# A graph network layer pair on Trainium2: unordered scatters of the edge list, and list steps tied behind given messages

## The chip, the cores and the metric

One core of a Trainium2 chip runs the whole program. The metric is the device time of one execution in microseconds. The engines are named as in the profile: PE (TensorE matmul; PEld its weight loads), DVE (VectorE), ACT (ScalarE), POOL (GpSimd) and SP (SyncE); SPq, ACTq and POOLq are the queues from which an engine issues DMAs.

## What is computed

There are 6250 nodes with 256 features and 106250 edges, sorted by destination; 6250 of them are self loops and the others come in both directions. Two layers run one after the other on the same edges. Layer 0 sends a message over each edge, which depends on the source node and on one of two edge types; layer 1 is a graph attention layer with four heads. Cut to what matters (`norm` is a layer norm without weights):

```python
def edge_nn(x, W, b):
    h = relu(x @ W.T + b)
    return relu(h @ W.T + b)
msgs = where(rel == r, edge_nn(x[src], W_rel[r], b_rel[r]), ...)   # r = 0, 1
agg = segment_sum(msgs, dst)
i, f, g, o = split(agg @ W_ih.T + b_ih + b_hh, 4)
hn = sigmoid(o) * tanh(sigmoid(i) * tanh(g))
x = norm(x + mlp3(hn))                       # three small dense layers
...
h = x @ W                                    # 4 heads of 64
e = leaky_relu(a_src[src] + a_dst[dst], 0.2)
alpha = softmax of e over the edges of each dst
y = norm_affine(segment_sum(alpha * h[src], dst) + bias + x)
x = norm(x + relu(y))
```

## The kernel before

The kernel has a first stage, which this change touches, and a long second part (`fast`), which it doesn't. (A slower path, `general`, is there for inputs whose edges aren't sorted as expected; the profiled run doesn't take it.)

**Messages.** A message depends on source and type only, so there are just 2 x 6250 different ones. They are computed once per node and type and stored in device memory as the table `parts0`. Nodes are taken in 49 blocks of 128 (`NB = 49`); a "message" below is the message block of one such block, both types. The loop at L1138 takes pieces of four blocks (`CHUNK = 4`); with 49 blocks the last piece has one. For each piece SP loads the transposed features `fxc` (L1141, three buffers), PE makes the hidden layer with eight products into `fph` (L1149), ACT adds the bias and applies relu (L1156); then for each block PE makes four products into `fpm` (L1163, two PSUM buffers), DVE adds the bias (`fms`, L1171, three buffers), ACT applies relu (L1174) and SP stores the block (L1176).

**The edge list.** Beside that, DVE takes the edge list apart. SP loads destinations, sources and types (L810 to L833). From L839 on DVE packs source, type and flags of an edge in one word, drops the self loops by moving the words left in seven rounds (the loop from L879, `frame` and `moved`), and works out where each block of 64 words goes (`place`). POOL then writes 21 groups of blocks (seven parts of the list by three blocks) to `packed` in device memory with indirect DMAs (L931). `packed` has been filled with zeros by a DMA from ACT (L805), and the blocks that the scatters write lie apart: blocks of odd and even rows go to two halves. SP reads the two halves back in six DMAs (L961, L965, L970: `both` and `low`). DVE joins them and splits the fields again (L975 to L1048): rows of the message table (`frow`), destinations (`list_f`), flags (`frel_f`), sources (`fsrc`), steps of the destination (`fstep`); SP stores the steps as `cuts` (L1034). PE turns these five lists with 35 transpositions (L1059), DVE copies the results to `fidx` (twice), `dstE`, `fmark` and `ffirst` (L1064, L1072). One small product (L1085, `low_p`) spreads the first destinations of the windows over the partitions, one (L1076) adds up checks. Seven more transpositions (L1129) turn `fslot`, ACT copies each to `rel_b` (L1133, two buffers) and SP stores it in `slots` (L1134).

**What sets the order.** In this first stage a scheduler puts the instructions of each engine in one fixed order when the program is built, and adds the waits that the data need; it starts from the program text, in which the whole list comes ahead of the messages. Each engine and each issuing queue works in its order: an instruction that waits holds up all that stand behind it. Two DMAs that write the same tensor are ordered, unless the program says that they need not be. The order of the second part is written out by hand.

**The second part.** After a branch on `odd_i`, 782 gathers on POOL (L1271) fetch rows of `parts0`, PE sums them by one-hot products (L1633), and the dense part of layer 0 follows in between; then 782 gathers of `rows` and the attention layer. The first gather waits for the last message store.

Of the kernel before, what the change touches and what calls it, by code (L numbers as in the profile page):

```python
# [42 lines left out]
P = 128  # L43
# [6 lines left out]
NB = -(-N // P)  # L50
# [6 lines left out]
CHUNK = 4  # L57
# [17 lines left out]
NC = -(-EC // CT)  # L75
# [628 lines left out]
def gnn_kernel(  # L704
# [26 lines left out]
    nc = tc.nc  # L731

    def at(ap, offset, dims):
        return bass.AP(tensor=ap.tensor, offset=ap.offset + offset, ap=dims)

    def rows(ap, n):

        return at(ap, 0, [[0, P], [1, n]])
# [4 lines left out]
    slots = dram.tile([NW, (WT + 1) * P], BF16, name="slots")  # L743
    cuts = dram.tile([(NC + 1) * CT, P], F32, name="cuts")
    kept = dram.tile([NG, P, 3 * D], F32, name="kept")
    packed = dram.tile([2 * BLOCKS, HB], I32, name="packed")
# [25 lines left out]
    with (  # L772
# [2 lines left out]
        tc.tile_pool(name="fmsgp", bufs=2, space=PSUM) as mps,  # L775
    ):
        WrT_s = mw.tile([P, 2, 2, D], F32, name="fWrT")
        nc.scalar.dma_start(WrT_s, WrT.rearrange("r (k p) f -> p r k f", p=P))
        brc = mw.tile([P, 2, 2], F32, name="fbrc")
        brr = mw.tile([P, 2 * D], F32, name="fbrr")  # L780
        with nc.allow_non_contiguous_dma(reason="bias vectors, one element a partition"):
            nc.scalar.dma_start(brc, br.rearrange("r (k p) -> p r k", p=P))
        nc.scalar.dma_start(brr, rows(br, 2 * D))
        zrow = mw.tile([1, D], F32, name="fzrow")
        nc.vector.memset(zrow, 0.0)
        nc.sync.dma_start(parts0[ZERO0 : ZERO0 + 1, :], zrow)

        with (
# [19 lines left out]
            rest = EC - (NC - 1) * CT  # L808
            whole = CT * P
# [43 lines left out]
            work = lp.tile([P, NC, P], F32, name="work")  # L853
# [25 lines left out]
            for b in range(7):  # L879
                s = 1 << b  # L880
# [44 lines left out]
            for b in range(3):  # L925
                nc.vector.tensor_scalar(
                    place[:, b, :], two_t, side, float(b), op0=OP.add, op1=OP.add
                )
            for k in range(NC):
                for b in range(3):  # L930
                    nc.gpsimd.indirect_dma_start(  # L931
                        out=packed,
                        out_offset=bass.IndirectOffsetOnAxis(ap=place[:CT, b, k : k + 1], axis=0),
                        in_=frame[:CT, k, b * HB : (b + 1) * HB],
                        in_offset=None,
                    )


# [15 lines left out]
            both = lp.tile([P, 2, NC, P + 1], I32, name="both")  # L954
            nc.gpsimd.memset(both[:, :, NC - 1, :], 0)
            low_2 = lp.tile([1, 2, NW + 1], I32, name="low_2")
            nc.gpsimd.memset(low_2, 0)
            rest = TC - (NC - 1) * CT
            for s in range(2):
                o = (s * BLOCKS + 1) * HB - 1  # L960
                nc.sync.dma_start(  # L961
                    both[:CT, s, : NC - 1, :],
                    at(packed, o, [[P, CT], [whole, NC - 1], [1, P + 1]]),
                )
                nc.sync.dma_start(  # L965
                    both[:rest, s, NC - 1, :],
                    at(packed, o + (NC - 1) * whole, [[P, rest], [1, P + 1]]),
                )
                with nc.allow_non_contiguous_dma(reason="the last edge before each window"):
                    nc.sync.dma_start(  # L970
                        low_2[:, s, 1:NW], at(packed, o + WT * P, [[0, 1], [WT * P, NW - 1]])
                    )

            low_r = lp.tile([1, NW + 1], I32, name="low_r")
# [31 lines left out]
            for none, to, of in (  # L1006
# [24 lines left out]
            steps = step[:, :, :P]  # L1031
            nc.vector.tensor_sub(steps[:CT], list_f[:CT, :, 1:], list_f[:CT, :, :P])
            nc.vector.tensor_scalar(work[:CT], steps[:CT], FAR, None, op0=OP.mult)
            nc.sync.dma_start(  # L1034
                cuts[: NC * CT, :].rearrange("(k p) e -> p k e", p=CT), work[:CT, :, :]
            )
            far = lp.tile([CT, P], F32, name="far")
            nc.vector.memset(far, FAR)
# [5 lines left out]


            dstE = lp.tile([P, COLS], F32, name="dstE")
            src0 = src1
            nc.vector.tensor_scalar(src0[:CT], src1[:CT], 1.0, None, op0=OP.subtract)  # L1048
            for to, of in (
                (idx0, row),  # L1050
                (dstE, list_f[:, :, 1:]),
                (mark, rel_f[:, :, :P]),
                (idx1, src0),
                (first, steps),
            ):
                for k0, kn in blocks_of(NC, 4):
                    pt = lps.tile([P, 4 * CT], F32, name="turned")
                    for k in range(kn):
                        nc.tensor.transpose(  # L1059
                            pt[:, k * CT : (k + 1) * CT], of[:CT, k0 + k, :], ident[:CT, :CT]  # L1060
                        )
                    n = min(kn * CT, COLS - k0 * CT)
                    if to is not mark:
                        nc.vector.tensor_copy(to[:, k0 * CT : k0 * CT + n], pt[:, :n])  # L1064
                        continue

                    to2, of2 = (
                        ap.rearrange("p (g j) -> p g j", j=2 * WT)
                        for ap in (mark[:, k0 * CT : k0 * CT + n], pt[:, :n])
                    )  # L1070
                    for a, b, c in ((0, 1, 0), (1, 2, WT), (2, WT + 1, 1), (WT + 1, 2 * WT, WT + 1)):
                        nc.vector.tensor_copy(to2[:, :, a:b], of2[:, :, c : c + b - a])  # L1072
# [9 lines left out]
            nc.vector.tensor_scalar(odd_i, odd[:, 6:7], 1.0, None, op0=OP.min)  # L1082

            low_p = lps.tile([P, NW + 1], F32, name="low_p", bufs=1)
            nc.tensor.matmul(low_p, ones[0:1, :], low, start=True, stop=True)  # L1085
            low_b = lp.tile([P, NW + 1], F32, name="low_b")
            nc.vector.tensor_copy(low_b, low_p)
            own = dstE[:, : NW * WT].rearrange("p (w j) -> p w j", j=WT)
# [37 lines left out]
            for w0, wn in blocks_of(NW, P // (WT + 1)):  # L1126
                pt = lps.tile([P, 4 * CT], F32, name="turned")
                n = wn * (WT + 1)
                nc.tensor.transpose(  # L1129
                    pt[:n, :P], slot[:, w0 : w0 + wn, :].rearrange("p w j -> p (w j)"), ident  # L1130
                )
                rel_b = lp.tile([P, P], BF16, name="rel_b", bufs=2)
                nc.scalar.copy(rel_b[:n, :], pt[:n, :P])  # L1133
                nc.sync.dma_start(  # L1134
                    slots[w0 : w0 + wn, :].rearrange("w (j e) -> (w j) e", e=P), rel_b[:n, :]
                )

        for b0, bn in blocks_of(NB, CHUNK):  # L1138
            cols = bn * P
            xc = mp.tile([P, 2, CHUNK * P], F32, name="fxc", bufs=3)  # L1140
            nc.sync.dma_start(  # L1141
                xc[:, :, :cols], xT[:, b0 * P : b0 * P + cols].rearrange("(k p) n -> p k n", p=P)
            )
            hT = mp.tile([P, 2, 2, CHUNK * P], F32, name="fhT")
            for r in range(2):
                for m in range(2):
                    ph = mps.tile([P, CHUNK * P], F32, name="fph")
                    for k in range(2):
                        nc.tensor.matmul(  # L1149
                            ph[:, :cols],  # L1150
                            WrT_s[:, r, k, m * P : (m + 1) * P],
                            xc[:, k, :cols],
                            start=(k == 0),
                            stop=(k == 1),
                        )
                    nc.scalar.activation(  # L1156
                        hT[:, r, m, :cols], ph[:, :cols], AF.Relu, bias=brc[:, r, m : m + 1]
                    )
            for j in range(bn):
                pm = mps.tile([P, 2, D], F32, name="fpm")  # L1160
                for r in range(2):
                    for k in range(2):
                        nc.tensor.matmul(  # L1163
                            pm[:, r, :],
                            hT[:, r, k, j * P : (j + 1) * P],
                            WrT_s[:, r, k, :],
                            start=(k == 0),
                            stop=(k == 1),
                        )
                ms = mp.tile([P, 2, D], F32, name="fms", bufs=3)  # L1170
                nc.vector.tensor_add(  # L1171
                    ms.rearrange("p r f -> p (r f)"), pm.rearrange("p r f -> p (r f)"), brr
                )
                nc.scalar.activation(ms, ms, AF.Relu)  # L1174
                b = b0 + j
                nc.sync.dma_start(  # L1176
                    parts0[2 * b * P : 2 * (b + 1) * P, :].rearrange("(p r) f -> p (r f)", r=2),
                    ms.rearrange("p r f -> p (r f)"),
                )

    odd_v = nc.values_load_multi_w_load_instructions(
        odd_i,
# [855 lines left out]
```

## Time and profile before

| what | us |
|---|---|
| timed, median of 3 runs (lowest, highest) | 2273.53 (2273.02, 2274.97) |
| the profiled execution, its own time | 3062.77 |
| its span, first to last instruction | 3061.0 |
| first product of the messages starts | 6.18 |
| first scatter to last scatter starts | 77.85 to 135.11 |
| list reload issues | 137.37 to 141.01 |
| last message product ends | 199.16 |
| first gather of layer 0 starts | 203.84 |
| last gather of layer 0, first gather of layer 1 | 1434.05, 1482.51 |
| last gather of layer 1 starts | 2969.30 |

The profiled execution is much longer than the timed ones. Its page gives busy time of each engine (PE 1529.9, DVE 1229.8, POOL 1527.2), groups of instructions with the idle time before them and what ended most of it, and the trace behind it answers with timelines and waits. A row of a timeline has the start, the duration, the engine, the line, the operation, what it writes and reads, how often, and in brackets the idle time before it with its releaser. Matmuls of 32-bit floats have two records each, so that `x16` are eight products.

### The profile page before, as it was taken

The numbers are of one execution on the slowest core, as the hardware profiler recorded it, in microseconds if no ns is written. First come the engines' busy times: TensorE is split into PE (matmuls) and PEld (weight loads), VectorE is DVE, ScalarE is ACT, GpSimd is POOL, SyncE is SP. The second block draws the span as 40 slices with busy tenths as digits, with TensorE's granted clock in tenths as the row PEclk, the third lists the DMA queues.
The fourth block names the chain that finished last, engine by engine and source line by source line (L and its number), as shares of the span: only waits on it lengthen the run. The fifth ranks groups of instructions, "written<-read, shape, count | busy, mean of one in ns | idle before, by whom it ended". The sixth has DMA issues, their size and how long they took to land. (4 is left out here: it accounts for less than half of the span.)

```text
span 3061.0 us, 22029 instructions
## 1 busy us (share of the span) xinstructions
PE 1529.9 (50%) x5722; PEld 792.0 (26%) x5722; DVE 1229.8 (40%) x3333; ACT 506.0 (17%) x1526; POOL 1527.2 (50%) x1603
## 2 busy tenths in 40 slices
PE   9871276767676756788223332423324233242344
PEld 5540132323233322334111111212112121121222
DVE  8240132322333233333114544535445354453656
ACT  3320011211121211134201111111111111111112
POOL 0227566666666666641473354553545545455440
PEclk9985688878788878889555665656656566565667
DMA  4343334444444434442342243342433334243330
GB/s 150 109 137 108 96 104 122 143 124 139 132 139 135 131 118 132 131 127 79 100 117 79 80 116 86 103 108 81 117 84 106 105 83 117 82 111 100 88 99 27
DMA packets 163393, 332.53 MB, mean 109 GB/s; under 512 B 42451, under 2 KB 74290, under 8 KB 163257
## 3 DMA queue, kind: packets, MB, share of 16 engines
q0 software_dynamic: 75968, 208.00, 24.6%
q1 hardware_dynamic: 64736, 82.92, 8.4%
q10 hardware_dynamic: 22553, 40.12, 4.3%
q8 instruction: 47, 0.77, 0.1%
q14 instruction: 89, 0.73, 0.1%
HBM read 278.79 MB, written 52.12 MB: 108 GB/s over the span
## 5 line engine op out<-in xcount | busy, mean ns | idle before, releaser
L1271 POOL DMA_INDIRECT G<-rows,fidx x782 | 743.9, 951 | 746.6 <-DVE gw L1818 513.3
L1271 POOL DMA_INDIRECT G<-parts,fidx x782 | 752.3, 962 | 483.9 <-issue 216.4
L1927 PE MATMUL fps<-gw,oh 128*64 128x264 f32 (+1 forms) x1674 | 448.2, 480 | 284.1 <-DVE gw L1818 218.1
L1633 PE MATMUL fps<-G,oh 128*64 128x257 f32 (+1 forms) x1674 | 465.2, 428 | 91.5 <-issue 49.7
L1927 PEld LDWEIGHTS fps<-gw,oh 128*64 128x64 f32 (+1 forms) x1674 | 233.9, 171 | 468.6 <-DVE gw L1818 231.7
L1818 DVE TENSOR_TENSOR gw<-G,bank 128x1792 f32<-128x1792 f32 (+1 forms) x167 | 249.1, 1491 | 169.8 <-issue 123.7
L1633 PEld LDWEIGHTS fps<-G,oh 128*64 128x64 f32 (+1 forms) x1674 | 204.1, 152 | 332.1 <-issue 219.8
L1777 PE MATMUL turn<-s,toward 120*120 120x1 f32 (+2 forms) x60 | 15.7, 331 | 435.9 <-DVE s L1774 432.4
L1486 PE MATMUL fpg<-faT,fWihT 128*128 128x512 f32 (+2 forms) x432 | 182.9, 549 | 49.2 <-issue 28.7
L1773 DVE TENSOR_TENSOR_SCAN s<-cut,turn 120x128 f32<-120x128 f32 (+2 forms) x30 | 12.6, 419 | 448.1 <-remote 442.6
L1439 DVE TENSOR_SCALAR kind<-fps 128x1 f32<-128x1 f32 x112 | 12.4, 152 | 359.6 <-PE fps L1633 183.8
L1454 PE MATMUL fpg<-fident,agg 128*128 128x128 f32 x112 | 29.2, 351 | 236.7 <-DVE agg L1443 132.7
L1354 DVE TENSOR_TENSOR oh<-bank,fslot 128x1024 f32<-128x1024 f32 x112 | 136.1, 1215 | 0.6 <-ACT bank L1797 0.6
L1777 PEld LDWEIGHTS turn<-s,toward 120*120 120x120 f32 (+2 forms) x60 | 13.2, 278 | 450.2 <-DVE s L1774 445.9
L1766 PE MATMUL turn<-fident,e 128*120 128x128 f32 (+2 forms) x30 | 13.5, 449 | 229.3 <-issue 214.6
L1594 DVE COPY nd<-hr 128x4 f32<-128x4 f32 x56 | 9.8, 176 | 242.6 <-ACT hr L1573 150.4
L1486 PEld LDWEIGHTS fpg<-faT,fWihT 128*128 128x128 f32 x432 | 73.8, 198 | 124.0 <-issue 96.7
L1149 PE MATMUL fph<-fxc,fWrT 128*128 128x512 f32 (+1 forms) x208 | 91.7, 589 | 6.3 <-DMA fWrT<-in_WrT_dram 6.2
L1163 PE MATMUL fpm<-fWrT,fhT 128*128 128x256 f32 x392 | 89.1, 381 | 0.6 <-DVE fms L1171 0.5
L1867 ACT ACTIVATE frs<-fmv,eps_c 128x1 f32<-128x1 f32 x112 | 33.0, 294 | 332.0 <-DVE fmv L1866 121.9
L1457 DVE COPY faT<-fpg 128x256 f32<-128x256 f32 x56 | 23.6, 422 | 157.0 <-remote 72.6
L1779 ACT COPY ends<-turn 120x2 f32<-120x2 f32 (+2 forms) x30 | 4.8, 159 | 493.2 <-PE turn L1778 478.1
(237 smaller groups left out, 1964.7 us busy)
## 6 DMA issues: line engine op xcount, KB each, us to landing
kept<-keep SPq DMA_DIRECT2D x56, 384.0 KB
k<-kept ACTq DMA_DIRECT2D x56, 384.0 KB
dB<-slots ACTq DMA_DIRECT2D x112, 128.0 KB
loop<-parts SPq DMA_DIRECT2D x110, 128.0 KB
parts<-fms SPq DMA_DIRECT2D x49, 256.0 KB
G<-parts,fidx POOLq DMA_INDIRECT x782
G<-rows,fidx POOLq DMA_INDIRECT x782
rows<-hr SPq DMA_DIRECT2D x110, 65.0 KB
```

The source lines that it names most:

```text
L1149: nc.tensor.matmul(ph[:, :cols], WrT_s[:, r, k, m * P : (m + 1) * P], xc[:, k, :cols], start=(k == 0), stop=(k == 1),)
L1163: nc.tensor.matmul(pm[:, r, :], hT[:, r, k, j * P : (j + 1) * P], WrT_s[:, r, k, :], start=(k == 0), stop=(k == 1),)
L1271: nc.gpsimd.indirect_dma_start(out=to_tile, out_offset=None, in_=table, in_offset=bass.IndirectOffsetOnAxis(ap=idx, axis=0),)
L1354: nc.vector.tensor_tensor(to[:, :nj, :], iota_s[:, None, :].to_broadcast([P, nj, SLOTS]), of[:, :, None].to_broadcast([P, nj, SLOTS]), op= ...
L1454: nc.tensor.transpose(pt[:, k * P : (k + 1) * P], agg[:, k * P : (k + 1) * P], ident)
L1457: nc.vector.tensor_copy(aT[:, :, i * P : (i + 1) * P], pt.rearrange("p (k n) -> p k n", k=2))
L1486: nc.tensor.matmul(pg[:, :cols], WihT_s[:, k, c * P : (c + 1) * P], aT[:, k, :cols], start=(k == 0), stop=(k == 1),)
L1633: nc.tensor.matmul(sums[g][to, :], ohj, got[t], start=begins, stop=ends)
L1777: nc.tensor.matmul(pd[:rs, 0:1], toward[:rs, 0, :rs], b[:, P - 1 : P], start=True, stop=True)
L1818: nc.vector.tensor_mul(gw[:, :, :D].rearrange("p j (h f) -> p j h f", h=H), of[:, :n, :D].rearrange("p j (h f) -> p j h f", h=H), ex[:, o ...
L1867: nc.scalar.activation(r, mv[u, k, 1:2], AF.Ln, bias=eps_c[u])
L1927: nc.tensor.matmul(sums[g][to, :], ohj, gw, start=begins, stop=ends)
```

## The change

It does these things:

- The weights `fWrT` are loaded in two DMAs, type 0 first, the biases between them; the table of ACT functions is loaded ahead of the first use (`preload_act_table_set`).
- The message loop begins with a piece of one block and goes on with twelve of four.
- The 21 scatters are declared free of order among themselves. The six DMAs of the reload are made to wait for all 21.
- Steps of the list get a place in the order of their queue or engine: the reload comes behind the store of message 29 (`NB - 20`), the store of `cuts` behind that of 38, the stores of `slots` behind that of 45; the transpositions of the five lists come behind the products of messages 35 to 39, and `low_p` behind those of 35. These ties (`NoSync`) set an order and add no wait of their own.
- `rel_b` has seven buffers instead of two.

```diff
@@ -775,12 +775,15 @@
         WrT_s = mw.tile([P, 2, 2, D], F32, name="fWrT")
-        nc.scalar.dma_start(WrT_s, WrT.rearrange("r (k p) f -> p r k f", p=P))
         brc = mw.tile([P, 2, 2], F32, name="fbrc")
         brr = mw.tile([P, 2 * D], F32, name="fbrr")
-        with nc.allow_non_contiguous_dma(reason="bias vectors, one element a partition"):
-            nc.scalar.dma_start(brc, br.rearrange("r (k p) -> p r k", p=P))
+        for r in range(2):
+            nc.scalar.dma_start(WrT_s[:, r, :, :], WrT[r].rearrange("(k p) f -> p k f", p=P))
+            if r == 0:
+                with nc.allow_non_contiguous_dma(reason="bias vectors, one element a partition"):
+                    nc.scalar.dma_start(brc, br.rearrange("r (k p) -> p r k", p=P))
         nc.scalar.dma_start(brr, rows(br, 2 * D))
+        nc.scalar.preload_act_table_set("exp_and_others")
@@ -926,13 +929,31 @@
+            moves, behind = [], []
             for k in range(NC):
                 for b in range(3):
-                    nc.gpsimd.indirect_dma_start(
+                    move = nc.gpsimd.indirect_dma_start(
                         out=packed,
...
                     )
+                    for other in moves:
+                        tc.declare_no_dep(move.ins, other.ins, reason="blocks of their own")
+                    moves.append(move)
+
+            def after_moves(load):
+                behind.append((NB - 20, load))
+                for move in moves:
+                    tc.add_manual_dep(
+                        load.ins,
+                        move.ins.name,
+                        mybir.DependencyInfo(
+                            mybir.DependencyClass.Sync, mybir.DependencyReason.DATA
+                        ),
+                        reason="the whole list",
                     )
@@ -958,17 +979,23 @@
-                nc.sync.dma_start(
-                    both[:CT, s, : NC - 1, :],
-                    at(packed, o, [[P, CT], [whole, NC - 1], [1, P + 1]]),
-                )
+                after_moves(
+                    nc.sync.dma_start(
+                        both[:CT, s, : NC - 1, :],
+                        at(packed, o, [[P, CT], [whole, NC - 1], [1, P + 1]]),
+                    )
+                )
...
@@ -1031,8 +1058,13 @@
-            nc.sync.dma_start(
-                cuts[: NC * CT, :].rearrange("(k p) e -> p k e", p=CT), work[:CT, :, :]
+            behind.append(
+                (
+                    NB - 11,
+                    nc.sync.dma_start(
+                        cuts[: NC * CT, :].rearrange("(k p) e -> p k e", p=CT), work[:CT, :, :]
+                    ),
+                )
             )
@@ -1056,9 +1089,11 @@
                     for k in range(kn):
-                        nc.tensor.transpose(
+                        turn = nc.tensor.transpose(
                             pt[:, k * CT : (k + 1) * CT], of[:CT, k0 + k, :], ident[:CT, :CT]
                         )
+                        late.append((turns // 2, turn))
+                    turns += 1
@@ -1082,7 +1117,7 @@
-            nc.tensor.matmul(low_p, ones[0:1, :], low, start=True, stop=True)
+            late.append((0, nc.tensor.matmul(low_p, ones[0:1, :], low, start=True, stop=True)))
@@ -1129,13 +1164,20 @@
-                rel_b = lp.tile([P, P], BF16, name="rel_b", bufs=2)
+                rel_b = lp.tile([P, P], BF16, name="rel_b", bufs=7)
                 nc.scalar.copy(rel_b[:n, :], pt[:n, :P])
...
+                behind.append(
+                    (
+                        NB - 4,
+                        nc.sync.dma_start(
+                            slots[w0 : w0 + wn, :].rearrange("w (j e) -> (w j) e", e=P),
+                            rel_b[:n, :],
+                        ),
+                    )
+                )
-        for b0, bn in blocks_of(NB, CHUNK):
+        for b0, bn in [(0, 1)] + [(1 + b, n) for b, n in blocks_of(NB - 1, CHUNK)]:
@@ -1160,7 +1202,7 @@
-                        nc.tensor.matmul(
+                        made = nc.tensor.matmul(
@@ -1173,10 +1215,24 @@
-                nc.sync.dma_start(
+                store = nc.sync.dma_start(
...
+                tied = [(NB - 14 + n, one, made) for n, one in late]
+                tied += [(n, one, store) for n, one in behind]
+                for n, one, sooner in tied:
+                    if b == n:
+                        tc.add_manual_dep(
+                            one.ins,
+                            sooner.ins.name,
+                            mybir.DependencyInfo(
+                                mybir.DependencyClass.NoSync, mybir.DependencyReason.DATA
+                            ),
+                            reason="the list comes late",
+                        )
```

More of the change, by code (lines that the diff above doesn't have):

```diff
@@ L960, in gnn_kernel @@
                 o = (s * BLOCKS + 1) * HB - 1
-                nc.sync.dma_start(
-                    both[:CT, s, : NC - 1, :],
-                    at(packed, o, [[P, CT], [whole, NC - 1], [1, P + 1]]),
-                )
-                nc.sync.dma_start(
-                    both[:rest, s, NC - 1, :],
-                    at(packed, o + (NC - 1) * whole, [[P, rest], [1, P + 1]]),
+                after_moves(
[3 more added lines that the diff above has]
+                    )
+                )
+                after_moves(
+                    nc.sync.dma_start(
+                        both[:rest, s, NC - 1, :],
+                        at(packed, o + (NC - 1) * whole, [[P, rest], [1, P + 1]]),
+                    )
                 )
                 with nc.allow_non_contiguous_dma(reason="the last edge before each window"):
-                    nc.sync.dma_start(
-                        low_2[:, s, 1:NW], at(packed, o + WT * P, [[0, 1], [WT * P, NW - 1]])
+                    after_moves(
+                        nc.sync.dma_start(
+                            low_2[:, s, 1:NW], at(packed, o + WT * P, [[0, 1], [WT * P, NW - 1]])
+                        )
                     )
@@ L1033, in gnn_kernel @@
             nc.vector.tensor_scalar(work[:CT], steps[:CT], FAR, None, op0=OP.mult)
-            nc.sync.dma_start(
-                cuts[: NC * CT, :].rearrange("(k p) e -> p k e", p=CT), work[:CT, :, :]
+            behind.append(
+                (
+                    NB - 11,
+                    nc.sync.dma_start(
+                        cuts[: NC * CT, :].rearrange("(k p) e -> p k e", p=CT), work[:CT, :, :]
+                    ),
+                )
             )
@@ L1046, in gnn_kernel @@
             dstE = lp.tile([P, COLS], F32, name="dstE")
+            late, turns = [], 0
             src0 = src1
@@ L1131, in gnn_kernel @@
                 )
-                rel_b = lp.tile([P, P], BF16, name="rel_b", bufs=2)
+                rel_b = lp.tile([P, P], BF16, name="rel_b", bufs=7)
                 nc.scalar.copy(rel_b[:n, :], pt[:n, :P])
-                nc.sync.dma_start(
-                    slots[w0 : w0 + wn, :].rearrange("w (j e) -> (w j) e", e=P), rel_b[:n, :]
+                behind.append(
+                    (
+                        NB - 4,
+                        nc.sync.dma_start(
+                            slots[w0 : w0 + wn, :].rearrange("w (j e) -> (w j) e", e=P),
+                            rel_b[:n, :],
+                        ),
+                    )
                 )
-        for b0, bn in blocks_of(NB, CHUNK):
+        for b0, bn in [(0, 1)] + [(1 + b, n) for b, n in blocks_of(NB - 1, CHUNK)]:
             cols = bn * P
@@ L1175, in gnn_kernel @@
                 b = b0 + j
-                nc.sync.dma_start(
+                store = nc.sync.dma_start(
                     parts0[2 * b * P : 2 * (b + 1) * P, :].rearrange("(p r) f -> p (r f)", r=2),
@@ L1179, in gnn_kernel @@
                 )
+                tied = [(NB - 14 + n, one, made) for n, one in late]
[9 more added lines that the diff above has]
+                            reason="the list comes late",
+                        )
     odd_v = nc.values_load_multi_w_load_instructions(
```

## The prediction

> **What bounds the kernel now.** I read the page first, for the shape of the whole. Two groups of gathers on POOL stand on top, 782 each:
>
> ```profile
> span 3061.0 us, 22029 instructions
> L1271 POOL DMA_INDIRECT G<-rows,fidx x782 | 743.9, 951 | 746.6 <-DVE gw L1818 513.3
> L1271 POOL DMA_INDIRECT G<-parts,fidx x782 | 752.3, 962 | 483.9 <-issue 216.4
> ```
>
> In the timeline of POOL undisturbed gathers start 1.25 us apart (204 on, 600 on, 1482 on). 1564 x 1.25 = 1955; with the first gather at 203.84, 47 us between the layers (1435 to 1482.5) and 91 us after the last gather (2970 to 3061) this makes 2297, against 2273.53 timed. So the timed runs have hardly any of the gathers' idle time that the profile has (3062.77 for that execution), POOL paces them nearly from 204 to the end, and what comes before the first gather stands wholly on the path. The change touches only that stretch, so the whole sum is made there. Next I read the timelines of PE, DVE, POOL and SP's queue from 0 to 205, then the queue's waits. PE:
>
> ```profile
> 6.18 9.20 PE L1149 MATMUL fph<-fxc,fWrT 128*128 128x512 f32 x16 [6.18 <-DMA fWrT<-in_WrT_dram]
> ...
> 99.30 7.07 PE L1163 MATMUL fpm<-fWrT,fhT 128*128 128x256 f32 x32
> ...
> 113.07 7.07 PE L1163 MATMUL fpm<-fWrT,fhT 128*128 128x256 f32 x32
> ...
> 133.75 1.88 PE L1149 MATMUL fph<-fxc,fWrT 128*128 128x512 f32 x4
> 146.39 0.77 PE L1085 MATMUL low_p<-low,fones 1*128 1x113 f32 x2 [10.76 <-DVE low L980]
> ...
> 158.34 0.97 PE L1059 MATMUL turned<-fident,frow 126*128 126x126 f32 x7 [0.82 <-DVE frow L1026]
> ...
> 197.27 1.89 PE L1163 MATMUL fpm<-fWrT,fhT 128*128 128x256 f32 x8
> ```
>
> A piece of four messages takes 13.77 us (99.30 to 113.07) and PE is dense, but for one hole of 10.76 (the bracket: idle time before the row, and what ended it). What made it, from the timelines of DVE and of POOL and the waits of SP's queue:
>
> ```profile
> 130.56 0.69 DVE L1171 TENSOR_TENSOR fms<-fpm,fbrr 128x512 f32<-128x512 f32 x1 [1.09 <-PE fpm L1163]
> 143.09 1.10 DVE L992 TENSOR_TENSOR both<-both 126x903 int32<-126x903 int32 x1 [11.84 <-DMA both<-packed]
> ...
> 158.22 0.14 DVE L1043 TENSOR_REDUCE bad<-same 126x1 f32<-126x7 f32 x1
> ```
> ```profile
> 77.85 1.16 POOL L931 DMA_INDIRECT packed<-frame,place  x1 [70.98 <-DVE fms L1171]
> 80.84 1.00 POOL L931 DMA_INDIRECT packed<-frame,place  x1 [1.83 <-DMA packed<-frame,place]
> ...
> 135.11 0.99 POOL L931 DMA_INDIRECT packed<-frame,place  x1 [1.51 <-DMA packed<-frame,place]
> 203.84 0.99 POOL L1271 DMA_INDIRECT G<-parts,fidx  x1 [67.74 <-ACT G L1654]
> ```
> ```profile
> SPq L961 <- DMA packed<-frame,place: 15.3, 1, 15.3
> ```
>
> Read backwards: PE waits for the list's lows from DVE, DVE for the list's reload, the reload (SP, 137.37 to 141.01) for the scatters, and each of 21 scatters for the one before to land: 57.3 us over 20 steps, 2.86 each, 2.46 where nothing else is in flight. The store of messages behind the reload waits too.
>
> PE's account: twelve pieces 165.2, the last one-message piece 4.4, the list's transpositions and small products 7.3; sum 176.9, against 193.0 from 6.18 to 199.16. The 16.1 between are 10.76 + 0.82 for the list, 2.3 of slow first matmuls (9.20 instead of 6.9), 1.3 at 41 while DVE unpacks, 0.9 of crumbs.
>
> **What the Trainium skill says.** "DMA: Bandwidth & Descriptors", section "Anatomy of one DMA — SWDGE (gpsimd) path": some 2.0 us fixed for each, mostly the receipt of the write, and the issuing sequencer does any waiting. The trace agrees in kind: 0.99 on POOL, then 1.5 or more of waiting. "TensorE: Matmul & The Clock Gate", "Part 1: The HAM clock gate": about the first 3.4 us run at half clock; here the first weight loads stand 0.86 apart until 10.0 and 0.43 later. "ScalarE: Activation LUTs", "What ACT_TABLE_LOAD costs": 1.28 us; the trace has 1.28, from 6.92.
>
> **The change, part by part**, with the instruction order of the built kernel beside the trace's durations.
>
> *Start.* The first piece has one message: its columns (128 KB) and half the weights (256 KB) instead of 512 KB each stand ahead of the first matmul. 1 MB landed at 6.18, some 5 us after issue; half of it, with a fixed part left, gives an estimate of 4.6. The piece takes 4.4 warm and 2.0 more for the slow clock: message 0 done at 11.0. The last piece now has four messages, so PE's work is the same. The preloaded table takes 1.28 off ACT, where it waited for the biases till 6.92 while PE needed it at 9.6 only: nothing, except for the small piece that needs it sooner. Against the gain: SP's fourth column load now waits for PE's first piece (about 9.2) and stands before the ten list loads, which started at 6.21. Unpacking on DVE then has no gain: 59.8 us of dense work (17.1 to 76.9), ended near 77 to 78 as before. PE loses some 1.9 to it. So the start brings about 1 us, between -2 and 2.
>
> *Scatters.* Twenty waits of 1.5 to 3.5 go[...]. The pitch becomes POOL's own, 1.25 as in the gathers: 20 x 1.25 = 25, so landed near 106 instead of 137. The trace has no unordered scatters of this kind; bounds are 1.25 and the old 2.86.
>
> *Reload.* Tied behind the store of message 29. Messages 0 to 32 end at T = 11.0 + 8 x 13.77 + 1.9 = 123.1; message 29 at 117.9, its store (sum, relu, 1.6) at 119.5; six issues of 3.6 (137.37 to 141.01) and 2.1 to land: 125.2. Behind them wait the stores of messages 30 to 32; sums have three buffers, and DVE turns to the list next, so nothing waits for these.
>
> *List on DVE.* In the new order it stands after the sum of message 32, 32 instructions in one block, 15.3 us as in the trace (143.09 to 158.36): 125.2 to 140.5. Then message 33's sum, 0.7. PE meanwhile has 8 first products (6.9), messages 33 and 34 (3.5) and 6 more first products (5.2), to T + 15.5 = 138.6, then needs that sum: a hole of 2.6 in place of 10.76 + 0.82.
>
> *Transpositions* stand behind messages 35 to 39, so each group finds DVE's input ready. Walking through in order, PE waits 0.2 for a copy and about 1.0 for the slots: copies between them are DVE work of 13.6 us, beside 15 us and more of PE's. If that cover were gone, 3 us. Their time on PE is unchanged. Stores of cuts and slots move back in SP's queue, behind messages 38 and 45; seven buffers let ACT go on, and they land well before the first gather.
>
> *Sum.* T + 4 pieces 55.1 + small products 7.0 + holes 3.8 = 189.0, against 199.16: 10 us in the profiled execution (3062.77 to 3053). After it, 4.7 us to the first gather, unchanged.
>
> For the timed runs I take less. The hole is made of the scatters' landing times. At the 2.46 that the trace shows without company they end 8 us sooner, and the hole shrinks from 10.8 to 2.8: the gain is then 2. The extra steps stand beside message loads and stores, which timed runs have too, so I expect most, not all, of the hole: 6.5 us, 2273.5 - 6.5 = 2267.0.
>
> **Rivals.**
> 1. *The hole is small in the timed runs* (scatters at 2.3 to 2.5): 0 to 4.5 gained, 2271. For it: 790 us of the profiled time are absent from timed runs, so the profile slows something. Against: the loads and stores of this stretch land within about 2 us even there.
> 2. *Scatters stay serial though nothing orders them* (the ring drains one at a time): the change then doesn't do what it says. SP reaches the reload at 119.5 and blocks, with every message store behind it. At 2.86 they land at 137.2, the list starts at 143, PE gets message 33's sum at 159 instead of 141: 18 later, 8 slower than before, 2281. It decides from a pitch of about 2.5 on. Against: gathers run at 1.25 with many in flight.
> 3. *The list comes too late at the start*: the blocked list loads hold unpacking up by 3 to 5 us, and PE idles with it; gain and loss cancel, 2273 to 2277.
>
> **How the numbers follow.** Forecast 0.55 (its own range 2263 to 2269), rival 1 0.33, rival 2 0.06, rival 3 0.06, of which a third beyond 0.2%. 0.2% is 4.5 us, about what a measurement of this kernel can tell from no change. Faster 0.55, same 0.37, slower 0.08. The range from 2263 to 2274.5 leaves out gains above 10.5 (0.06), rival 2 and half of rival 3.
>
> **What would show it.** In the profile after: 21 scatters 1.25 to 1.4 apart, ended before 110; reload near 120 without a wait; low product after message 35 without a wait; one PE hole of 2 to 4 us near 139; first gather near 194. Wrong if scatters stay near 2.5, if the first gather moves by under 3 us, or if the unpack ends after 80. If the first gather is 10 sooner and the time isn't, the hole was the profiler's.

## The result, and the profile after

| what | before | after |
|---|---|---|
| timed, median of 8 runs each (lowest, highest), us | 2275.27 (2273.02, 2277.97) | 2268.24 (2265.01, 2271.69) |
| ratio to before, 95% interval | | 0.9969 (0.996 to 0.9979) |
| profiled execution, own time and span, us | 2276.0, 2274.2 (taken again, e0 below) | 2266.64, 2264.7 |
| first scatter to last scatter starts | 77.97 to 136.28 | 78.33 to 104.34 |
| list reload issues | 138.53 to 142.16 | 121.28 to 125.03 |
| last message product ends | 200.36 | 190.25 |
| first gather of layer 0 starts | 205.04 | 194.91 |

The change gained 7.0 us (4.8 to 9.1 by the interval). The kernel before takes some 2275 us in some executions and 3050 to 3060 in others (its first profile, and six of the twelve runs below), so each time is set only against the runs of before made beside it, whose median is given.

From the page of after, the span and the two groups of gathers (busy, mean ns, idle before them):

```profile
span 2264.7 us, 22022 instructions
L1327 POOL DMA_INDIRECT G<-parts,fidx x782 | 747.1, 955 | 327.5 <-issue 219.0
L1327 POOL DMA_INDIRECT G<-rows,fidx x782 | 747.5, 956 | 240.5 <-issue 222.9
```

The gathers idle 568 us here, where the first profile of before had 1230: this span is near the timed runs, that one was not. The timeline of POOL (start, duration, and in brackets the idle time before the row):

```profile
78.33 1.21 POOL L937 DMA_INDIRECT packed<-frame,place  x1 [71.54 <-DVE frame L902]
79.84 0.99 POOL L937 DMA_INDIRECT packed<-frame,place  x1 [0.30 <-issue]
...
104.34 0.98 POOL L937 DMA_INDIRECT packed<-frame,place  x1 [0.30 <-issue]
194.91 0.99 POOL L1327 DMA_INDIRECT G<-parts,fidx  x1 [89.58 <-ACT G L1710]
```

Twenty steps take 26.0 us, 1.30 each, in place of 58.3 in e0. No scatter's bracket names a landing any more. SP's queue and then DVE, both from their timelines:

```profile
120.63 0.33 SPq L1218 DMA_DIRECT2D parts<-fms  x1
121.28 0.35 SPq L983 DMA_DIRECT2D both<-packed  x1
```
```profile
124.49 0.69 DVE L1213 TENSOR_TENSOR fms<-fpm,fbrr 128x512 f32<-128x512 f32 x1 [1.03 <-PE fpm L1205]
127.20 1.10 DVE L1019 TENSOR_TENSOR both<-both 126x903 int32<-126x903 int32 x1 [2.02 <-DMA both<-packed]
...
142.39 1.27 DVE L1213 TENSOR_TENSOR fms<-fpm,fbrr 128x512 f32<-128x512 f32 x2
```

The reload follows the store of message 29 at once, and no wait for the scatters is left among the waits of SP's queue. DVE waits 2.0 for the rows instead of 12.9 (e0; 11.8 in the first profile of before), then makes no sum until 142.39. What that does to PE, from its timeline:

```profile
4.72 3.78 PE L1191 MATMUL fph<-fxc,fWrT 128*128 128x128 f32 x16 [4.72 <-DMA fWrT<-in_WrT_dram]
...
134.55 5.31 PE L1191 MATMUL fph<-fxc,fWrT 128*128 128x512 f32 x12
143.12 3.11 PE L1205 MATMUL fpm<-fWrT,fhT 128*128 128x256 f32 x8 [3.25 <-DVE fms L1213]
146.02 1.52 PE L1092 MATMUL turned<-fident,frow 126*128 126x126 f32 x7
147.47 0.47 PE L1120 MATMUL low_p<-low,fones 1*128 1x113 f32 x2
...
183.18 7.07 PE L1205 MATMUL fpm<-fWrT,fhT 128*128 128x256 f32 x32
```

One hole of 3.25 is left, with another releaser: not the list itself, but the sum of message 33, which stands behind the list on DVE. The small product and the transpositions, which waited 10.76 and 0.82 in the first profile of before, follow without a bracket.

### The profile page after: what moved, and what is told of

It reads as the page before. It is cut to its first block, busy times and chain, and to the rows that moved or that the text cites. A ratio compares the mean times of both kernels' runs of the same rounds, so it can differ in the third digit from the quotient of the medians.

```text
span 2264.7 us, 22022 instructions
## 1 busy us (share of the span) xinstructions
PE 1556.6 (69%) x5722; PEld 776.5 (34%) x5722; DVE 1237.3 (55%) x3333; ACT 508.5 (22%) x1526; POOL 1525.5 (67%) x1603
## 3 DMA queue, kind: packets, MB, share of 16 engines
q1 hardware_dynamic: 64736, 82.92, 11.4%
## 5 line engine op out<-in xcount | busy, mean ns | idle before, releaser
L1689 PE MATMUL fps<-G,oh 128*64 128x257 f32 (+1 forms) x1674 | 533.1, 433 | 137.1 <-DMA G<-parts,fidx 120.6
L1983 PE MATMUL fps<-gw,oh 128*64 128x264 f32 (+1 forms) x1674 | 433.0, 469 | 238.3 <-DVE gw L1874 238.3
L1689 PEld LDWEIGHTS fps<-G,oh 128*64 128x64 f32 (+1 forms) x1674 | 196.6, 151 | 445.5 <-DMA G<-parts,fidx 226.7
L1495 DVE TENSOR_SCALAR kind<-fps 128x1 f32<-128x1 f32 x112 | 12.5, 153 | 311.1 <-PE fps L1689 311.1
L1542 PE MATMUL fpg<-faT,fWihT 128*128 128x512 f32 (+2 forms) x432 | 171.6, 521 | 0.2 <-DVE faT L1513 0.2
L1929 ACT ACTIVATE fy<-fy,frs 128x256 f32<-128x256 f32 x112 | 67.2, 600 | 98.4 <-DVE gw L1868 52.9
L1205 PEld LDWEIGHTS fpm<-fWrT,fhT 128*128 128x128 f32 x392 | 74.9, 194 | 23.8 <-DVE fms L1213 8.8
L1873 ACT COPY gw<-bank 128x28 f32<-128x28 f32 (+1 forms) x167 | 28.5, 171 | 227.6 <-DMA dB<-slots 103.6
L1625 PE MATMUL fpg<-Wx,fyT 128*128 128x264 f32 x224 | 77.0, 474 | 3.0 <-ACT fyT L1616 3.0
L937 POOL DMA_INDIRECT packed<-frame,place x21 | 20.9, 995 | 77.6 <-DVE frame L902 71.5
```

Of the source, the lines that this page charges most:

```text
L1205: made = nc.tensor.matmul(pm[:, r, :], hT[:, r, k, j * P : (j + 1) * P], WrT_s[:, r, k, :], start=(k == 0), stop=(k == 1),)
L1542: nc.tensor.matmul(pg[:, :cols], WihT_s[:, k, c * P : (c + 1) * P], aT[:, k, :cols], start=(k == 0), stop=(k == 1),)
L1625: nc.tensor.matmul(ph[u, :], hs[i][:, k, u], Wx[:, k, :], start=(k == 0), stop=(k == 1))
L1689: nc.tensor.matmul(sums[g][to, :], ohj, got[t], start=begins, stop=ends)
L1873: nc.scalar.copy(gw[:, :, D:HA], ex[:, o : o + n, :])
L1929: nc.scalar.activation(y, y, AF.Identity, bias=m, scale=r)
```

## The experiments

The theory: serial scatters held the reload, the reload the list, the list PE; without their order, and with the list placed where it arrives, the hole goes. Rivals: the small first piece makes the gain; the ties alone make it; the hole was the profiler's.

**e0: the kernel before, profiled again.** No edit.

> The kernel before, profiled again. Theory (the hole behind the chain of scatters is the kernel's own): a profile whose span is near the timed runs shows the scatters 2.5 to 2.9 us apart, the hole of TensorE ahead of the message that follows the list, 9 to 11 us, and the first gather near 203.8, as in the first profile. Rival 1 (the hole was made by the profiled execution, which was 800 us long later on): scatters closer together, a hole under 6 us, first gather near 200 or earlier, and then the change could only gain its start. Time: the same as before, ratio 1.000.

2276.73 us beside 2275.98 of before, ratio 1.0004 (0.9995 to 1.0012). From the timelines of PE and of DVE, and one line of the waits over the first 205 us (total, times, longest):

```profile
147.59 0.76 PE L1085 MATMUL low_p<-low,fones 1*128 1x113 f32 x2 [11.85 <-DVE low L980]
148.29 11.54 PE L1149 MATMUL fph<-fxc,fWrT 128*128 128x512 f32 x20
159.66 0.92 PE L1059 MATMUL turned<-fident,frow 126*128 126x126 f32 x7
```
```profile
144.29 1.10 DVE L992 TENSOR_TENSOR both<-both 126x903 int32<-126x903 int32 x1 [12.93 <-DMA both<-packed]
```
```profile
POOL packed L931 <- DMA packed<-frame,place: 38.4, 20, 3.6
```

The profiled execution took 2276.0 us, a usual time, and has the hole in full, with scatters 2.92 apart and the first gather at 205.04. So the hole belongs to the kernel; rival 1 of the prediction falls.

**e1: unordered scatters alone.** Before, with this and with the reload's waits for all scatters:

```diff
+                    for other in moves:
+                        tc.declare_no_dep(move.ins, other.ins, reason="blocks of their own")
+                    moves.append(move)
```

> Only the mutual order of the scatters goes; no ties, no small first piece. The schedule then puts the list reload on the sync engine earlier, behind the store of message 20, where it blocks until the scatters have landed. Theory (scatters are the cause, ties keep the two sides in step): scatters 1.3 us apart, landed near 107, list rows in near 113; TensorE waits some 4 us for low and 3 us for the list's rows; first gather near 199, 4 to 5 us sooner than before: ratio 0.998. Rival (the small first piece makes the gain): ratio 1.000. Rival (the ties make it): ratio 1.000 or above. If the unordered scatters are the whole of it: 0.997 as the full change.

2282.9 us beside the same 2275.98, ratio 1.003 (1.0018 to 1.0041): 6.9 us slower. The theory (0.998) fails, and so does the rival of the small piece (1.000); the rival of the ties (1.000 or above) covers it, and e3 below tests that one. Timelines of DVE and of PE:

```profile
111.72 1.10 DVE L1007 TENSOR_TENSOR both<-both 126x903 int32<-126x903 int32 x1 [20.00 <-DMA both<-packed]
```
```profile
115.02 0.76 PE L1100 MATMUL low_p<-low,fones 1*128 1x113 f32 x2 [18.07 <-DVE low L995]
```

The scatters start 1.3 apart and end 33 us sooner, and the rows are there at 111.7 instead of 144.3. But without the scatters' order the schedule puts the list further forward on each engine: SP comes to the reload near 87 and waits 18.9, DVE after 23 sums and waits 20.0, PE after 24 messages, at 96.95, and waits 18.1. The list came 32.6 us earlier, its place on PE 38.8 earlier (135.74 to 96.95); the 6.2 between them are what the hole grew by. My expectation had the place right and PE's time there wrong by 15 us: 24 messages at 3.44 from 10 on and 4.3 of first products end at 97, not at the 112 that a wait of 4 us for rows in near 113 would need.

**e3: ties and small piece, scatters in order.** The full change without the first two of the lines shown in e1, so that the scatters keep their order.

> The full change with the scatters in mutual order again. Theory: the ties let the list wait no less, since the scatters land at 138 to 141 whatever the sync engine does; the reload that now stands behind the store of message 29 holds the stores queued behind it, and the list comes in at about 144: first gather near 211, 7 us later than before, ratio 1.003. Rival (the ties or the small first piece make the gain): ratio 0.997 to 0.999.

2281.12 us beside 2275.98, ratio 1.0024 (1.0015 to 1.0033): 5.1 us slower, near the 1.003 expected. Timelines of DVE and of PE:

```profile
145.00 1.10 DVE L1017 TENSOR_TENSOR both<-both 126x903 int32<-126x903 int32 x1 [20.14 <-DMA both<-packed]
```
```profile
160.92 3.78 PE L1203 MATMUL fpm<-fWrT,fhT 128*128 128x256 f32 x8 [16.22 <-DVE fms L1211]
```

The first gather is at 208.53. So the ties and the small piece don't gain without the unordered scatters; the place is right only for a list that comes early.

**e5: the full change without ties.** The condition `if b == n` made false.

> The full change without the ties: unordered scatters and the small first piece, the schedule free to place the reload and the transpositions. It puts the reload behind the store of message 20 and the transpositions behind message 25. Theory: holes of TensorE of about 4 us (low) and 3 us (list rows) in place of one of 3.3 us; first gather near 198, 3 us later than with the ties, ratio to before 0.9975. Rival (the ties do nothing): ratio 0.997 as the full change and the first gather near 195. Rival (the ties are the main part): ratio 0.999 to 1.001.

2283.29 us beside 2275.98, ratio 1.0031 (1.0019 to 1.0043), first gather 212.68. From the timeline of PE:

```profile
118.10 0.76 PE L1120 MATMUL low_p<-low,fones 1*128 1x113 f32 x2 [18.57 <-DVE low L1007]
```

It is e1 again, with the small piece: without the ties there is no gain at all. The expectation had the same error as e1's.

Beside the next four, before takes 3059.44 us. **a: the changed kernel again.** No edit.

> The changed kernel, profiled and timed again, as the reference of the others of this chip. Expected: first gather near 195, 9 to 10 us ahead of the second profile of before (205.0), ratio 0.996 to 0.998. Rival (the first profile of after was a lucky one, and the timed difference of 7.0 us is what the change moves): first gather near 197 to 198.

3068.66 us, ratio 1.0024 (1.0005 to 1.0044): here the change doesn't gain, it loses a little. The first gather stands at 208.49, where theory and rival had 195 and 197 to 198 and the first profile of before 203.84. The timeline of DVE shows why:

```profile
91.92 0.69 DVE L1213 TENSOR_TENSOR fms<-fpm,fbrr 128x512 f32<-128x512 f32 x1 [7.85 <-PE fpm L1205]
97.95 0.69 DVE L1213 TENSOR_TENSOR fms<-fpm,fbrr 128x512 f32<-128x512 f32 x1 [5.33 <-remote]
107.78 1.45 DVE L1213 TENSOR_TENSOR fms<-fpm,fbrr 128x512 f32<-128x512 f32 x2 [9.14 <-remote]
```

Two sums wait 14.5 us for something that the trace doesn't name, the second until 107.78, when the scatters (the last issued at 104.60) have ended; PE stops for 3.36 and 4.71 there and for 3.48 at the list. The first profile of after has no such waits.

**e2: no small piece.** In the changed kernel `for b0, bn in blocks_of(NB, CHUNK)` and the single load of `WrT_s` again, no preload.

> The full change with the first piece of four messages, the weights in one load and no preload, as before: unordered scatters and all ties stay. Theory (the start is worth 1 to 2 us and the scatters the rest): first gather near 197, 2 us after the full change, ratio to before 0.997 to 0.998. Rival (the small first piece makes most of the gain): first gather at 201 or later, ratio 0.999 or above. Rival (it does nothing, the hole grows by what the start gains): first gather near 195, ratio as the full change.

3067.33 us, ratio 1.0029 (1.0008 to 1.0051), like the full change beside it (3068.66). First gather 212.46, 4.0 later, but PE's holes sum to 15.7 instead of 12.6, and the difference lies in the unnamed waits (11.4 instead of 8.1): the start isn't isolated.

**e4: the small piece alone.** e2's edit the other way round, in the kernel before.

> The kernel before with the small first piece, the weights in two loads and the preload, nothing else. Theory (the serial scatters set when the list comes, and TensorE waits for the list, so what the start gains goes into that wait): hole of 11 to 14 us, first gather 204 to 207, ratio 0.9995 to 1.001. Rival (the small first piece makes the gain): first gather 202 or sooner, ratio 0.998 or below.

3060.36 us, ratio 1.0006 (0.9985 to 1.0027), hole 11.91 ahead of `low_p`. The hole stays, as expected; a gain of 2 us can't be told here, where the interval is 13 us wide. The scatters began at 80.84 and the first gather came at 206.83, both 3 us later than in the first profile of before (77.85 and 203.84): the piece alone brought nothing to the list.

**t1: no ties of the transpositions.** `tied = []` for the late ties of the changed kernel.

> The full change without the ties of the transpositions and of low_p; the ties of the reload and of the later stores stay. The schedule then keeps the reload behind the store of message 29 and the list behind 33 sums, and puts low_p some 3 messages sooner, behind message 32 and most of a piece of first products. Theory A (the tie of the reload is the one that acts, since it sets where the list stands on VectorE): hole of 3 to 4 us, ahead of the first transposition in place of the message product, first gather within 1 us of the full change, ratio 0.997. Theory B (TensorE's own ties act): low_p waits 5 us or more, first gather 5 us or more later than the full change, ratio 0.999 or above.

3063.25 us, ratio 1.0017 (0.9994 to 1.004), first gather 207.89, 0.6 ahead of the full change beside it. `low_p` waits 0.39, the first transposition 2.68. That fits theory A in the traces (its ratio of 0.997 not, as in a): the ties of the transpositions change nothing that can be seen once the reload, and with it the list on DVE, has its place. In the built order the list stands behind 33 sums in t1 and behind 23 in e5, so it is the tie of the reload or those of the later stores that act; the tie of the reload was not taken out by itself.

Beside the next two, before takes 3050.19 us. **g8: the list between sums.** In the changed kernel, with names for five operations of the list and for the sum:

```diff
-                behind.append((NB - 20, load))
+                behind.append((NB - 22, load))
...
-                tied = [(NB - 14 + n, one, made) for n, one in late]
+                tied = [(NB - 12 + n, one, made) for n, one in late]
...
+                tied += [(NB - 17, lists_low, summed), (NB - 16, lists_part, summed), (NB - 15, lists_row, summed), (NB - 14, lists_rel, summed), (NB - 17, lists_or, summed)]
```

> A further step from the changed kernel: the reload stands two stores sooner on the sync engine (behind message 27), the first two operations of the list are tied behind the sum of message 32, the middle of the list behind the sums of 33, 34 and 35, and the transpositions two messages later. The whole computation is done. Theory (what is left of TensorE's hole, 3.3 us, is the list's 15 us block on VectorE, in which no sum of a message is made, so that TensorE runs out of accumulators): with three sums inside the block and the rows there before it, the 2.0 us wait for the rows and the hole of 3.3 us go; last message product ends near 187, first gather near 192, 3 us ahead of the changed kernel; ratio to before 0.995 to 0.997. Rival (the list then ends later by the three sums and TensorE waits as long for the list's rows): hole of 2 to 4 us ahead of the first transposition, first gather near 195, ratio as the changed kernel.

3049.5 us, ratio 1.0005 (0.9989 to 1.0022), first gather 203.44, against 0.995 to 0.997 and 192 expected. The unnamed waits are there again (9.22 on PE near 110); at the list a hole of 0.94 is left.

**e2b: e2 again.**

> The full change without its small first piece, split weights and preload, again: the run of it before this one stood in executions of 3060 us[...]. Theory: first gather near 197, 2 us after the changed kernel (194.9), ratio to before 0.997 to 0.998. Rival (the start makes most of the gain): first gather at 201 or later, ratio 0.999 or above. Rival (the start does nothing): first gather near 195.

3055.55 us, ratio 1.0021 (1.0004 to 1.0038), first gather 211.50, PE stopped 11.24 and 3.20: e2 repeated, and the start still not isolated. Beside a before of some 2275 us, the full change without its small piece was not run.

**h2 and h1: more buffers, and two chains**, beside a before of 2276.36 us. h2 is g8 with `bufs=8` for `fms`; h1 is g8 with `for other in moves[-1:]`.

> The list between the sums as in g8, and one size changed: eight buffers in place of three for the sum of a message, from which its store is made. The order of instructions on every engine stays. The whole computation is done. Theory (in the runs of some 3050 us TensorE's hole of 9 to 15 us near 98 to 110 comes from stores whose landing is held up while the scatters run without mutual order; the sum of a message waits for the landing of the store three messages back): with eight buffers the sums don't wait, that hole is gone, and the first gather lies near 192 to 194 in such a run too; ratio to before 0.995 to 0.998. Rival (the sums wait for something else that is slow in these runs): the hole stays at 9 us or more, first gather near 203. Where the run is one of some 2270 us, which showed no such hole, both say the first gather near 192 and a ratio of 0.995 to 0.996.

> The list between the sums as in g8, and the scatters in two chains: each waits for the landing of the one two before it, and only neighbours have no mutual order. Pitch from the ordered one (2.94 us, of which 1.97 is the wait for the landing): half of that, 1.5 us, so landed near 111, before the reload at 113. The whole computation is done. Theory (in runs of some 3050 us it is the many scatters in flight at once that hold the stores): the hole near 98 to 110 is gone or under 3 us, first gather near 192 to 196. Rival (any scatters without order hold the stores, or the pitch does): the hole stays at 6 us or more, first gather at 200 or later. Where the run is one of some 2270 us: pitch 1.5 us, first gather near 192, ratio 0.995 to 0.996.

h2: 2263.86 us, ratio 0.9945 (0.9932 to 0.9958), first gather 191.81. h1: 2262.76 us, ratio 0.9945 (0.9933 to 0.9957), first gather 192.18. In h1 the two chains didn't come about: the built program is the same as g8's, and the scatters are 1.30 apart with no wait for a landing. So it is a run of g8. Its timeline of PE:

```profile
139.24 5.31 PE L1191 MATMUL fph<-fxc,fWrT 128*128 128x512 f32 x12
145.49 1.98 PE L1191 MATMUL fph<-fxc,fWrT 128*128 128x512 f32 x4 [0.94 <-ACT fhT L1198]
```

The hole goes from 3.25 to 0.94, and the first gather is 2.7 to 3.1 us ahead of that of the changed kernel. g8 does two things for it: three sums stand inside the list's block on DVE, and the reload, two stores sooner, has the rows there in time (DVE's wait of 2.02 for them is gone). Which of the two gives how much wasn't taken apart. The version gains 13.6 us (h1) and 12.5 us (h2); their intervals end at 0.9958 and that of the change begins at 0.996, though each stands against its own runs of before. Eight buffers bring nothing over three here. Whether they cover the unnamed waits was the question, and these runs had none: it stays open.

## Why the prediction was right, by its steps

| step | predicted | measured |
|---|---|---|
| first product; message 0 done | 4.6; 11.0 | 4.72; 11.4 |
| unpacking ends | 77 to 78 | 78.5 |
| pitch of the scatters | 1.25 | 1.30 |
| message 32 ends (T) | 123.1 | 124.4 |
| reload's first issue | 119.5 | 121.28 |
| list on DVE | 125.2 to 140.5 | 127.20 to 142.4 |
| PE's hole | 2.6 | 3.25 |
| last product; first gather | 189.0; near 194 | 190.25; 194.91 |
| timed | 2267.0 | 2268.24 |

**Scatters, reload, list, hole: right.** The pitch is what POOL needs for itself, 0.99 and 0.30. The Trainium skill's "DMA: Bandwidth & Descriptors", section "Anatomy of one DMA — SWDGE (gpsimd) path", puts most of a DMA's fixed 2.0 us in the completion, and the trace agrees: a wait of 1.92 in the mean (38.4 over 20 in e0) shrinks to 0.30 without the order. The delays of 1 to 2 us in the table come from T, 1.3 late, and with it the reload, 1.8 late. The waits of 1.2 that I gave PE among the transpositions didn't come: its rows there have no bracket. From the last product to the first gather it is 4.7 in both profiles, as taken.

**Start: mis-sized, within its bounds.** I took a gain of 1 us; it is about 0.2. PE starts 1.68 sooner, but waits 1.27 and 0.53 for sums while DVE unpacks, where e0 waits 0.49. A piece of one message takes 4.36 (e0's last, 196.00 to 200.36), a piece of four 13.77. By these, after has 114.5 of work done at T, 124.39, and e0 123.9 when its 36th message is done, at 134.03: 9.9 and 10.1 over. No run isolates the start in the time, and no effect of it shows between the profiles: the nine with the small piece are 9.5 to 11.3 over at message 20, four without it 10.0 to 10.7 at message 23 (e2 is left out, as its unnamed waits have begun by then).

**The sum in the profile: 10 us predicted, 10.1 measured at the last product and at the first gather.** Of these the holes are 8.6 (11.85 to 3.25). Another 1.2 I hadn't named: after a hole the products run slow. In e0 the small product and the 20 records behind it take 12.1 to the start of the next row instead of 9.0 at the dense rate; in after the first 8 take 2.9 instead of 1.7 and the next 7 1.45 instead of 0.76, together 1.9 more. TensorE's granted clock in the traces, as a share of full speed, shows why: it is 0.50 from 140.1 to 153.7 in e0 and from 143.8 to 147.3 in after, and 1.00 on either side; it stays at 1.00 through the hole of 0.94 in h1. The Trainium skill's "TensorE: Matmul & The Clock Gate", section "Part 1: The HAM clock gate", says that the clock halves after an idle window of some 3.4 us; the hole of 11.85 agrees, and the one of 3.25, though a little under it, was followed by the half clock too, so here the measurement goes before the figure. 8.6, 1.2 and the start's 0.2 make 10.0 of the 10.1.

The last product came 1.25 later than the 189.0 of my sum, as late as T. Behind T two errors cancelled, which is luck: the slow products, 1.9, which I had put at nothing, and the small products, some 5.7 by what is left of the stretch instead of 7.0 (the durations that I had added up overlap), together with the holes, 3.25 instead of 3.8.

**First gather to end: unchanged.** Span less first gather is 2069.2 in e0, 2069.7 in e1, 2069.6 in e3, 2069.7 in e5, 2069.8 in after: what lies before the first gather is on the path, to within 0.6 us. The 2297 of my account came out too long because I took the 91 us after the last gather from the long profile; in e0 it is 66, which makes 2273.

**The discount was argued wrongly.** I took 6.5 of 10 because the hole might be shorter in timed runs. e0 shows it in full in an execution of usual length; that 6.5 lies near the measured 7.0 is luck. From profile to profile the time falls by 9.4 (2276.0 to 2266.64); the medians fall by 7.0, with 9.1 as the interval's end. After's runs spread over 6.7 us and the profiled one is the third lowest of eight; what makes the other 2 us isn't settled.

**Rivals.** Rival 2's case, serial scatters under ties, was built as e3, there by order. It put the sum of message 33 at 159, measured 160.2, and the time at 2281, measured 2281.12; but that was 8 above a before of 2273.5, and e3 is 5.1 above 2275.98, so the number met by luck. Rival 3 didn't come: unpacking ended at 78.5. Missing from my list was the one that e1 and e5 show: with the ties gone the same early list costs 7 us. Missing too was the case of a, in which sums wait for something else while the scatters run.

## What to carry to other kernels

A wait costs the distance between where an instruction stands in its engine's order and when its data come; making the data earlier helps only if the place stays, and a scheduler may move it: e1 had the list 33 us sooner and lost 7. Change cause and place together, and read the new order engine by engine before putting a price on it. Then look for what is late next, here a 15 us block on DVE with no sums inside.

## What the hardware showed that I had not expected

Of the six runs of 3050 to 3060 us, all five with unordered scatters have PE stopped for 8 to 12 us between 95 and 111, with DVE's sums waiting up to 9.2 for a release that the trace mostly doesn't name and that comes about when the scatters end; e4, with ordered ones, has no such stop. Sums have three buffers, so the completion of an earlier store is a candidate. In run a, the core's DMA moved 26 GB/s and less from 101.3 to 110, so hardly any of a store's data can have been moving then, which would point to a late completion; and where a wait of a sum near 50 us is named, in e5 and g8, it is one of 1.15 and 1.31 for a store (`DMA parts<-fms`). That is argued, not shown: no run tells what holds the sums.

The record names the chip of each of the twelve runs: the six of 3050 to 3060 us ran on two chips and the other six on two others, and the one program of g8 and h1 took 3049.5 us on one (ratio 1.0005) and 2262.76 us on another (0.9945), as the changed kernel had 0.9969 at first and 1.0024 in a. So a gain of 0.3 to 0.5% found on one chip need not hold on the next; what differs between them no run tells.
